# Layer 0's expert products on 64-row TensorE tiles, in two halves around the second scores of a turn

## The chip, the cores and the metric

The kernel runs on one NeuronCore of a Trainium2 chip. The core has TensorE (PE; its weight loads are listed apart as PEld), VectorE (DVE), ScalarE (ACT), GpSimd (POOL) and SyncE (SP, here the issuer of most DMAs). [...] The metric is the device time of one execution in microseconds.

## The reference

Two layers run over x of 16 batches x 512 tokens x 128 channels. In each, the attention part and the feed-forward part read the same normalised x, and their outputs are added to x.

```
xn = layernorm(x)
x  = x + L0_attn(xn) + L0_ffn(xn)      # L0_attn: a memory updated by gradient steps over 8 chunks
xn = layernorm(x)                      # L0_ffn: conv, 16-head attention, norm, 8 dense experts, norm
x  = x + L1_attn(xn) + L1_ffn(xn)      # L1_attn: two causal 16-head attentions with a conv between
                                       # L1_ffn: top 8 of 32 experts, capacity 128
```

The part that the change touches is the dense mixture of layer 0. For each token it is

```
gates = softmax(x1 @ gate_w + gate_b)                       # 8 experts, all are used
y = sum over e of gates[e] * (relu(x1 @ w1[e] + b1[e]) @ w2[e] + b2[e])
```

with w1[e] of 128 x 512 and w2[e] of 512 x 128. Per batch of 512 tokens this is 8 experts, each with two products of 512 x 128 x 512. Everything is fp32.

## The kernel before, in words

**Turns.** The program is written as Python generators ("stages") that a small planner (`Turns.run`, L280) steps once per turn. A stage has a starting turn and a level. In a turn all live stages are stepped in order of level. Level 0 is `tops` with `largest` (L374): the first scores, whose row maxima VectorE takes. Level 1 is `back` with `weighted` (L423): the second scores, their exp on ScalarE, and the products of the exps with the values. Level 2 finishes an attention (`summed`), levels 3 and 4 hold the scan, the projections and norms, and level 6 is `experts0`, the experts of layer 0. TensorE's queue follows this written order (`ORDERED`, L634). The other engines are ordered by the compiler's scheduler, with two written constraints: VectorE's work of level 1 and above stays behind the maxima of the turn (`newest`), and GpSimd's of level 2 and above behind the causal masking (`cleared`).

**Attention.** A head has 8 channels, split into a high and a low part, with the maxima as extra rows. Heads lie in two groups of 64 partitions, so the scores are float32r products on 64-row tiles, one per row group, in pairs (L388 and L465). Layer 0 takes 512 columns a turn. Layer 1 is causal and takes 512, 384, 2 x 256 or 4 x 128 columns, 11 turns for four heads of each row group. The exps are multiplied with the values on 128*32 tiles, four heads beside each other (`values`, L432), several turns later and by four or eight heads at a time (`tail`, L448).

**PSUM.** `pools["ps"]` has eight banks: five slots called `bank`, handed out by `work` (L177), one pair for the second scores (`p2`), one for the value sums (`ctx`). `held` counts the slots kept beyond a turn.

**Experts before.** `ffn(b)` (L530) works on one batch at a time. Its gate is a generator of its own that advances one step per turn. `first(i)` is one 128*128 product of w1 with all 512 tokens (tile phe) and a Relu on ScalarE into hTe. `second(i)` is four 128*128 products of hTe with w2 into pye, which is summed over four units in one bank, multiplied by the gate on ScalarE (L601) and added to `ac` on GpSimd (L602). After the first, units are listed alternately. How many run in a turn is decided by `credit`: each turn adds TURN = 2750 less `load_ns`, an account of the other products of the turn; a unit costs 1000. Units go in pairs, and in turns with value products none go unless more than three are due. They stand last in the turn.

**After the experts.** `middle(b)` waits for the experts of its batch and begins layer 1 for it, one batch per 44 turns. The 32 experts of layer 1 (`moe`) come at the end.

Of the kernel before, what the change touches and what calls it, by code (L numbers as in the profile page):

```python
# [17 lines left out]
P = 128  # L18
# [64 lines left out]
def network(ctx: ExitStack, tc: tile.TileContext, a, out):  # L83
# [39 lines left out]
    gw0 = load(const, "gw0", [P, EXP0])  # L123
# [62 lines left out]
    load_ns, look_ns, array_ns, at_ffn = [0.0], [0.0], [0.0], [-9]  # L186

# [85 lines left out]
    class Turns:  # L273
# [6 lines left out]
        def run(self, until=None):  # L280
            while (self.stages or self.live) and (until is None or not until()):
# [8 lines left out]
                with ExitStack() as behind:  # L290
                    if newest[0] is not None:
                        behind.enter_context(tc.issue_after(newest[0].ins))
                    left += [x for x in self.live if x[0] == 1 and step(x)]
                    if cleared[0] is not None:
                        behind.enter_context(tc.issue_after(cleared[0].ins))
                    left += [x for x in self.live if x[0] > 1 and step(x)]
# [126 lines left out]
    def weighted(slot, vp, c, causal, cn, name):  # L423
# [33 lines left out]
        for i, (kt, n, per, t) in enumerate(widths(causal)):  # L457
# [4 lines left out]
            for u in range(per):  # L462
                for r in range(2):
                    rr = slice(64 * r, 64 * r + 64)
                    mm(sv[:, r, u, :], k[rr, t + u, kt * P : (kt + 1) * P], q[rr, t + u, S - n :])  # L465
            tail(pools["heads"])
# [45 lines left out]
    credit, fetched = [0.0], {}  # L512

    def fetch1(w1, w2, e):
        w1[e] = ff.tile([P, DFF], F32, tag="ew1", bufs=2, name="ew1")
        nc.sync.dma_start(w1[e], a["ew1"][:, e, :])
# [5 lines left out]
    def fetch0(b):  # L522

        x1T = ff.tile([P, S], F32, tag="x1T", bufs=1, name="x1T")
        nc.sync.dma_start(x1T, x1d[1, b])
# [4 lines left out]
    def ffn(b):  # L530
# [12 lines left out]
        def gate():  # L543
            yield from room()
            pgt = hold("pgt")[:, 0 : TB * EXP0].rearrange("p (t e) -> p t e", e=EXP0)
            for t in range(TB):
                mm(pgt[:, t, :], x1T[:, t * P : (t + 1) * P], gw0)
# [22 lines left out]
            y = ff.tile([P, TB, D], F32, tag="y", bufs=2, name="y")  # L570
            nc.scalar.copy(flat(y), pb2)
            nc.gpsimd.tensor_tensor(ac, ac, y, ALU.add)
            yield

        hs, pye, n = {}, [None], 4 * EXP0

        def first(i):
            e, f = divmod(i, 4)
            if e + 1 < EXP0 and f < 2:
                (fetch1, fetch2)[f](w1, w2, e + 1)  # L580
            ph = work("phe")
            mm(ph, w1[e][:, f * P : (f + 1) * P], x1T)
            hs[i] = ff.tile([P, S], F32, tag="hTe", bufs=3, name="hTe")
            nc.scalar.activation(hs[i], ph, AF.Relu, bias=col("fb", i))  # L584
            if i == n - 1 and ("x1", b + 1) in done:
                fetch0(b + 1)

        def second(i):
            e, f = divmod(i, 4)
            h = hs.pop(i)  # L590
            if f == 0:
                pye[0] = toks(hold("pye"))
            for t in range(TB):
                nc.tensor.matmul(  # L594
                    pye[0][:, t, :], lhsT=h[:, t * P : (t + 1) * P], rhs=w2[e][:, f, :],
                    start=(f == 0 and t == 0), stop=(f == 3), skip_group_check=True,
                )
            if f == 3:
                y = ff.tile([P, TB, D], F32, tag="y", bufs=2, name="y")
                for t in range(TB):  # L600
                    nc.scalar.mul(y[:, t, :], pye[0][:, t, :], pr[:, t, e : e + 1])  # L601
                nc.gpsimd.tensor_tensor(ac, ac, y, ALU.add)  # L602
                drop()

        units = [(first, 0)]
        for i in range(1, n):
            units += [(first, i), (second, i - 1)]
        units.append((second, n - 1))
        gating, at = gate(), 0
        while at < len(units):  # L610

            at_ffn[0] = clock[0]
            credit[0] = min(credit[0] + TURN - load_ns[0], 4000)
            more = int(max(credit[0] + 500, 0) // 1000)
            if pools["pairs"]:
                more = more // 2 * 2 if "values" not in locks or more > 3 else 0
            if credit[0] > -2000:

# [984 lines left out]
```

## Time and profile before

| | us |
|---|---|
| runs shown, median (lowest to highest) | 3695.77 (3691.05 to 3702.05) |
| profiled execution, its own time | 3697.03 |
| profiled execution, span of its instructions | 3695.3 |
| TensorE matmuls busy | 3466.2 |
| VectorE busy | 2283.0 |
| ScalarE busy | 2154.0 |
| GpSimd busy | 1571.3 |
| first pye matmul to last | 280.4 to 3104.1 |

Groups of the experts over the whole trace (count, mean of one): phe matmuls of 512 columns, 1024, 612 ns; pye matmuls of 128 columns, 4096, 281 ns; Relu hTe, 512, 690 ns; multiply y, 512, 368 ns; add to ac, 128, 1285 ns. A product in fp32 appears as two passes, each with its own weight load, so 512 phe products make 1024 rows. A float32r product appears as one.

How to read it: a row of the timeline has the start, the length, the engine, the line, the tiles (out<-in), the shape of the TensorE tile as rows*columns, and the count of instructions merged in it. Rows of matmuls overlap, since they include the way through the array. In the groups, the busy time and the mean in ns follow the bar, then the idle time before them and what ended it.

### The profile page before, as it was taken

The page shows a single profiled execution, that of the slowest core. Times are in us where ns is not written, and L with a number is a line of the kernel's source. Part 1 is how long each engine was busy: PE and PEld are TensorE (multiplying, and loading weights), DVE is VectorE, ACT ScalarE, POOL GpSimd, SP SyncE. Part 2 cuts the span into 40 slices and gives each one's busy share as a digit, 9 for nine tenths or more (in the row PEclk, how much of TensorE's full clock was granted, in tenths as well). Part 3 has the DMA queues.
Part 4 walks back from the last instruction along what each step waited for, and adds up shares of the span by engine and source line. Part 5 has one row for each costly group of instructions (what it writes and reads, how often), then busy time and mean ns, then how long its engine had stood idle before and what let it go on. Part 6 is the DMA issues. An engine that isn't in the chain of part 4 may idle for free. (4 is left out here: it accounts for less than half of the span.)

```text
span 3695.3 us, 62879 instructions
## 1 busy us (share of the span) xinstructions
PE 3466.2 (94%) x22209; PEld 1925.9 (52%) x22209; DVE 2283.0 (62%) x5907; ACT 2154.0 (58%) x3703; POOL 1571.3 (43%) x2524
## 2 busy tenths in 40 slices
PE   6999999899999899999999999999999999998877
PEld 3445554454555455455555555555555665443443
DVE  5676656556756565566466666666666666777652
ACT  1556756665656687666566666666666665443433
POOL 5433532442431455432444344434443444443664
PEclk7999999899999999999999999999999999998998
DMA  5222222222223233443434443444344334333343
GB/s 171 68 69 74 80 77 65 68 74 82 65 66 94 85 114 93 122 120 105 135 96 132 121 125 110 120 124 127 101 124 130 114 107 116 96 99 95 84 85 85
DMA packets 290074, 370.83 MB, mean 100 GB/s; under 512 B 46016, under 2 KB 141408, under 8 KB 289376
## 3 DMA queue, kind: packets, MB, share of 16 engines
q1 hardware_dynamic: 282592, 359.99, 34.0%
q0 software_dynamic: 7168, 6.82, 1.1%
q8 instruction: 177, 2.90, 0.3%
q14 instruction: 137, 1.12, 0.1%
HBM read 236.85 MB, written 133.25 MB: 100 GB/s over the span
## 5 line engine op out<-in xcount | busy, mean ns | idle before, releaser
L470 ACT ACTIVATE e<-s 128x1024 f32<-128x1024 f32 (+1 forms) x1216 | 1190.9, 979 | 667.7 <-PE s L196 587.0
L399 DVE TENSOR_REDUCE nm<-s 128x1 f32<-128x512 f32 (+2 forms) x1408 | 906.9, 683 | 527.0 <-PE s L196 525.6
L391 DVE CUSTOM_DVE_ANT_0 s<-s,sb_const 128x512 f32<-128x512 f32 (+1 forms) x1024 | 624.3, 643 | 444.3 <-PE s L196 436.3
L474 POOL TENSOR_SCALAR_AFFINE_SELECT e<-e 128x128 f32<-128x128 f32 (+2 forms) x1408 | 467.0, 367 | 865.9 <-ACT e L470 859.5
L196 PE MATMUL s<-kx,qx 64*128 64x512 f32 (+3 forms) x3072 | 657.3, 430 | 58.8 <-DVE nm L399 14.6
L196 PE MATMUL pc<-e,vp 128*32 128x512 f32 (+3 forms) x6144 | 657.2, 506 | 43.9 <-POOL e L474 41.8
L196 PEld LDWEIGHTS s<-kx,qx 64*128 64x128 f32 x3072 | 293.1, 187 | 627.9 <-issue 251.9
L594 PEld LDWEIGHTS pye<-ew,hTe 128*128 128x128 f32 x4096 | 517.7, 192 | 174.0 <-issue 159.5
L196 PE MATMUL s<-qx,kx 64*128 64x512 f32 (+3 forms) x3072 | 533.2, 360 | 39.4 <-ACT e L470 27.6
L594 PE MATMUL pye<-ew,hTe 128*128 128x128 f32 x4096 | 564.6, 281 | 0.8 <-ACT hTe L584 0.8
L196 PE MATMUL phe<-x1T,ew 128*128 128x512 f32 x1024 | 539.9, 612 | 8.4 <-DVE nm L399 6.4
L584 ACT ACTIVATE hTe<-phe,sb_cols 128x512 f32<-128x512 f32 x512 | 352.8, 690 | 280.5 <-PE phe L196 278.3
L602 POOL TENSOR_TENSOR ac<-ac,y 128x512 f32<-128x512 f32 x128 | 164.5, 1285 | 408.8 <-ACT y L601 380.9
L196 PEld LDWEIGHTS s<-qx,kx 64*128 64x128 f32 x3072 | 294.6, 189 | 82.0 <-ACT e L470 57.0
L398 DVE TENSOR_TENSOR s<-s,sb_const 128x256 f32<-128x256 f32 (+1 forms) x384 | 180.9, 516 | 230.6 <-PE s L196 224.9
L196 PEld LDWEIGHTS pc<-e,vp 128*32 128x32 f32 x6144 | 155.5, 110 | 285.5 <-issue 173.1
L196 PEld LDWEIGHTS phe<-x1T,ew 128*128 128x128 f32 x1024 | 157.7, 192 | 59.8 <-issue 34.2
L601 ACT ACTIVATE y<-pye,pr 128x128 f32<-128x128 f32 x512 | 146.8, 368 | 30.8 <-PE pye L594 25.8
L203 PE MATMUL fill<-sb_pb,sb_const 128*128 128x512 f32 (+2 forms) x324 | 148.4, 547 | 10.9 <-DMA sb_pb<-in_pb 10.3
L391 DVE DVE_READ_ACCUMULATOR2_ANT nm<- 128x1 f32 x1024 | 144.6, 141 | 0.0
L209 POOL TENSOR_SCALAR rs_t<-ss 128x4 f32<-128x4 f32 (+1 forms) x56 | 11.9, 213 | 238.8 <-ACT sq L262 235.1
L209 POOL TENSOR_SCALAR rs_t<-ln_mv 128x4 f32<-128x4 f32 x64 | 12.7, 198 | 178.7 <-DVE ln_mv L219 176.4
(292 smaller groups left out, 3856.0 us busy)
## 6 DMA issues: line engine op xcount, KB each, us to landing
ew<-in_ew SPq DMA_DIRECT2D x256, 256.0 KB
kx<-rk SPq DMA_DIRECT2D x192, 256.0 KB
qx<-rq SPq DMA_DIRECT2D x128, 256.0 KB
rq<-hi SPq DMA_DIRECT2D x64, 256.0 KB
rq<-lo SPq DMA_DIRECT2D x64, 256.0 KB
rk<-hi SPq DMA_DIRECT2D x64, 256.0 KB
rk<-lo SPq DMA_DIRECT2D x64, 256.0 KB
qx<-r SPq DMA_DIRECT2D x64, 256.0 KB
```

Source lines behind the costliest of these rows:

```text
L196: nc.tensor.matmul(o, lhsT=lhsT, rhs=rhs, start=start, stop=stop)
L203: nc.tensor.matmul(o[:, 0:n], lhsT=ident, rhs=cell[0][:, 0:n], start=True, stop=True)
L209: nc.gpsimd.tensor_scalar(t, src, scale, eps, ALU.mult, ALU.add)
L391: newest[0] = nc.vector.tensor_tensor_reduce(out=sv[r][:, 0, :], in0=sv[r][:, 0, :], in1=row["caus"][:, S - n :], scale=1.0, scalar=-BIG, ...
L398: nc.vector.tensor_tensor(dg, dg, bc(row["caus"][:, S - P :], 1, per), ALU.add)
L399: newest[0] = nc.vector.tensor_reduce(nm[:, qt, r, t : t + per], sv[r], AX.X, ALU.max)
L470: nc.scalar.activation(e[:, :, 0 : per * n], s[:, :, 0 : per * n], AF.Exp, scale=SCALE)
L474: cleared[0] = nc.gpsimd.affine_select(out=ev[:, r, :, 0:P], in_=ev[:, r, :, 0:P], pattern=[[0, per], [1, P]], compare_op=ALU.is_ge, fill= ...
L584: nc.scalar.activation(hs[i], ph, AF.Relu, bias=col("fb", i))
L594: nc.tensor.matmul(pye[0][:, t, :], lhsT=h[:, t * P : (t + 1) * P], rhs=w2[e][:, f, :], start=(f == 0 and t == 0), stop=(f == 3), skip_gro ...
L601: nc.scalar.mul(y[:, t, :], pye[0][:, t, :], pr[:, t, e : e + 1])
L602: nc.gpsimd.tensor_tensor(ac, ac, y, ALU.add)
```

## The change

Experts run on 64*128 tiles. For `first`, w1 is laid out so that each group of 64 partitions holds another block of 128 hidden columns, and x1T is loaded twice, once for each row group: the 128 channels are contracted in two steps h = 0, 1. For `second`, each row group contracts its 64 of the 128 hidden rows and sums over the four blocks in a bank of its own. ScalarE multiplies the sum of one bank by the gate, VectorE that of the other, and GpSimd adds both to `ac`. A unit is now (`first` or `second`, expert, half p), 32 per batch instead of 64, and costs 2000 of credit.

A unit is a generator with one yield in its middle. `experts(True)` starts one between levels 0 and 1, if the last turn's credit was over 1000 (`due`), fewer than two slots are held, and, for `second`, the gate has finished (`ready`). `experts()` inside `weighted`, after the second scores and before the value products, runs the rest. At most one unit runs in a turn, in turns with values too. The gate's products use row group 0 alone, in two steps. `y` has half-size tiles, hTe four buffers for three, and some tiles of layer 1 change their pools or tags.

```diff
+    units, running, due, credit = [], [], [False], [0.0]
+    def experts(begin=False):
+        if running:
+            for _ in running.pop():
+                pass
+        elif begin and due[0] and units and held[0] - read[0] < 2:
+            fn, e, p, ready = units[0]
+            if fn.__name__ == "first" or ready:
+                units.pop(0)
+                running.append(fn(e, p))
+                next(running[0])
+                due[0] = False
+                credit[0] -= 2000
...
+                    experts(True)
                     left += [x for x in self.live if x[0] == 1 and step(x)]
+                    experts()
...
                     mm(sv[:, r, u, :], k[rr, t + u, kt * P : (kt + 1) * P], q[rr, t + u, S - n :])
+            experts()
             tail(pools["heads"])
...
-        x1T = ff.tile([P, S], F32, tag="x1T", bufs=1, name="x1T")
-        nc.sync.dma_start(x1T, x1d[1, b])
+        x1T = ff.tile([P, 2, S], F32, tag="x1T", bufs=1, name="x1T")
+        for g in range(2):
+            nc.sync.dma_start(x1T[64 * g : 64 * g + 64], x1d[1, b].rearrange("(h k) s -> k h s", h=2))
...
             for t in range(TB):
-                mm(pgt[:, t, :], x1T[:, t * P : (t + 1) * P], gw0)
+                for h in range(2):
+                    mm(pgt[:, t, :], x1T[0:64, h, t * P : (t + 1) * P], gw0[:, h, :], h == 0, h == 1)
...
-        def first(i):
+        def first(e, p):
+            banks = work("phe"), work("phe")
+            for h in range(2):
+                if p == 0 and e + 1 < EXP0:
+                    (fetch1, fetch2)[h](w1, w2, e + 1)
+                for g in range(2):
+                    rr = slice(64 * g, 64 * g + 64)
+                    nc.tensor.matmul(
+                        banks[g], lhsT=w1[e][rr, h, p, :], rhs=x1T[rr, h, :], start=(h == 0), stop=(h == 1),
+                    )
+                if h == 0:
+                    yield
+            for g in range(2):
+                f = 2 * p + g
+                hs[f] = ff.tile([P, S], F32, tag="hTe", bufs=4, name="hTe")
+                nc.scalar.activation(hs[f], banks[g], AF.Relu, bias=col("fb", 4 * e + f))
...
-        def second(i):
+        def second(e, u):
+            banks = [toks(work("pye")) for _ in range(2)]
+            two = slice(2 * u, 2 * u + 2)
+            for i in range(2):
+                t = 2 * u + i
+                for f in range(4):
+                    for g in range(2):
+                        rr = slice(64 * g, 64 * g + 64)
+                        nc.tensor.matmul(
+                            banks[g][:, i, :], lhsT=hs[f][rr, t * P : (t + 1) * P], rhs=w2[e][rr, f, :],
+                            start=(f == 0), stop=(f == 3),
+                        )
+                if i == 0:
+                    yield
+            y = [ff.tile([P, 2, D], F32, tag="y", bufs=2, name="y") for _ in range(2)]
+            for i in range(2):
+                t = 2 * u + i
+                nc.scalar.mul(y[0][:, i, :], banks[0][:, i, :], pr[:, t, e : e + 1])
+            nc.vector.tensor_tensor(y[1], banks[1][:, 0:2, :], bc(pr[:, two, e], 2, D), ALU.mult)
+            for g in range(2):
+                nc.gpsimd.tensor_tensor(ac[:, two], ac[:, two], y[g], ALU.add)
...
             credit[0] = min(credit[0] + TURN - load_ns[0], 4000)
-            more = int(max(credit[0] + 500, 0) // 1000)
-            if pools["pairs"]:
-                more = more // 2 * 2 if "values" not in locks or more > 3 else 0
...
-            next(gating, None)
+            due[0] = credit[0] > 1000
+            if next(gating, True):
+                ready.append(True)
             yield
```

## The prediction

> **What bounds the kernel now.** I read the page first, then the busy time by stretch, then TensorE's timeline inside one turn, then the waits and the groups by shape. TensorE leads the page:
>
> ```profile
> span 3695.3 us, 62879 instructions
> PE 3466.2 (94%) x22209; PEld 1925.9 (52%) x22209; DVE 2283.0 (62%) x5907; ACT 2154.0 (58%) x3703; POOL 1571.3 (43%) x2524
> ```
>
> By stretch (span cut where layer 0's experts begin, where the scan ends, where the experts end, and where the last `middle` starts):
>
> ```profile
> core 0: us, PE busy (x) PEld busy (x) DVE busy (x) ACT busy (x) POOL busy (x), PEclk, DMA share, GB/s
> 270.00:1530.00 1260.00, 1186.18 (x6856) 648.15 (x6860) 772.19 (x1397) 819.33 (x1600) 509.84 (x496) 0.97 0.28 81
> 1530.00:3110.00 1580.00, 1552.50 (x11052) 918.18 (x11044) 968.64 (x2948) 977.25 (x1563) 653.25 (x1335) 1.00 0.41 118
> 3110.00:3290.00 180.00, 166.89 (x1147) 81.17 (x1147) 134.02 (x414) 87.97 (x110) 74.48 (x188) 0.93 0.40 106
> ```
>
> From 1530 to 3110 us TensorE is busy 98% while VectorE, ScalarE and GpSimd stand at 61, 62 and 41%. So time there is TensorE's time. But its busy rows hide holes. The timeline of two turns, matmuls alone (start, length, ..., count):
>
> ```profile
> 1515.28 0.40 PE L196 MATMUL s<-qx,kx 64*128 64x512 f32 x2
> 1515.60 1.16 PE L594 MATMUL pye<-ew,hTe 128*128 128x128 f32 x8
> 1516.60 1.02 PE L196 MATMUL phe<-x1T,ew 128*128 128x512 f32 x2
> 1517.55 0.51 PE L196 MATMUL s<-kx,qx 64*128 64x512 f32 x2
> 1517.89 0.40 PE L196 MATMUL s<-qx,kx 64*128 64x512 f32 x2
> 1518.21 1.06 PE L196 MATMUL pc<-e,vp 128*32 128x512 f32 x8
> 1519.21 0.50 PE L196 MATMUL s<-kx,qx 64*128 64x512 f32 x2
> ```
>
> Compare ends, since every row carries the same pipeline tail. In unbroken stretches consecutive starts give 0.112 us for a 128-column fp32 pass, 0.43 for a 512-column one (each fp32 matmul is two passes), about 0.23 for a pair of 512-column scores. Scores end at 1515.68 and the eight pye passes at 1516.76: 1.08 for 0.90 of work, so **0.20 us lost** entering 128*128. pye to phe (1517.62) is 0.86 for 0.86: nothing lost. phe to the next scores (1518.06) is 0.44 for 0.23: **0.21 lost** leaving. Scores to scores (1518.29): nothing. Scores to pc: 1519.27, 0.98 for 0.86, 0.12 lost; pc to scores 0.21. So it is the change of tile shape that costs. Measured this way over the whole trace: 64*128 to 128*128 694 times, median 0.200; 128*128 to 64*128 1038 times, median 0.211.
>
> **The change, part by part.**
>
> *Shape switches.* I split TensorE's rows into runs of one shape. 283 runs of 128*128 between scores hold nothing but pye and phe; 39 more follow pc. (150 hold experts and other products, 556 only others; those switches stay.) With the experts on 64*128 the 283 runs vanish, 283 x 0.41 = 116; the 39 lose one switch of two, 39 x 0.20 = 8. **-124 us.** No trace shows fp32 and the scores' float32r alternating in one shape: the price is 0 to 0.20 a switch. I take 0, by pye to phe and pc to pye: same number type with another shape cost 0.20, same shape nothing.
>
> *Array work.* One new unit (a `first` or `second`) replaces one old first plus one old second on average: 512 of them. A `first` is two pairs of products (h = 0, 1; one of each row group), and if the two row groups overlap, 4 pair-passes x 0.43 = 1.72, as two old phe products (4 passes). A `second` is 16 pair-passes x 0.112 = 1.79, as two old pye. Row groups overlap in float32r (the x2 score rows last 0.40, not 0.62, and four-head 128-column score pairs start 0.112 apart, weight loads included); two-pass fp32 overlaps between column tiles (pc, four heads, eight passes: 1.06). The combination is in no row. Here a rule speaks against the change: the Trainium skill, "TensorE: Matmul & The Clock Gate", Part 3, says matmuls start and end in strict order. Then passes a, b of group 0 come before a of group 1: a half of `first` takes three slots, not two, +0.43 x 512 halves = 220, and a half of `second` nine for eight, +0.11 x 512 = 57: +277 us. By that rule pc's eight passes would need five slots, 2.3 us; the row says 1.06. I take the row: 0.
>
> *Banks.* The skill's "TensorEngine Tiling (Array Packing)", Restrictions and Gotchas, Gotcha 1, warns that row tiles write different PSUM banks, so pressure rises. Here: five `bank` slots; the first scores hold two, a unit now two at once (an old one one, and pye one over four turns), so one is spare. By the switches alone the sum below would be -120; with the rule I step one turn. Let t=0 be the end of the second scores in a turn with a `first` and nothing after it. exp starts at 0.20 (its row 1515.71 after scores whose rows end at 1515.68, tail of 0.17 taken off) and the next ScalarE instruction 0.91 later; the second half ends at 0.86; so Relu of group 0 runs 1.11 to 1.80 and its bank is free at about 1.88. TensorE reaches the next unit's first half at 0.86 + 0.23 = 1.09 and lacks one bank: **0.79 late**; with the 384-wide exp (0.81) 0.58. After a `second` (0.37 on ScalarE, 0.42 on VectorE) banks are free at 1.56: 0.47, or 0.26. Mean 0.52. Group 1's matmul blocks all behind it: second scores, values, the next exp. It takes units in consecutive turns, with no values or other product between. Values run in 4 turns of 11 in layer 1 (heads are popped by eights), and credit (+2750 less a turn's loads, -2000 a unit, due over 1000) drops after a unit in a turn with values, so that the next turn stays empty. Stepping it by hand through such cycles gives 3.5 consecutive cases and 2.5 empty turns followed by a unit in 11 turns. 558 turns from 1530 to 3110 make 178 and 127; a quarter of turns have other products, which leaves 134 x 0.52 = **+70**. After an empty turn the bank comes from VectorE's first maximum, 0.20 + 0.69 + 0.14 + 0.08 = 1.11 after the first scores, and TensorE is there after 2 x 0.23: 0.6 late, 95 x 0.6 = **+57**. The kernel before keeps units out of turns with values and has next to no empty turns: its 558 turns (exps counted) hold 466 runs of 128*128 and 91 returns from pc straight to scores. The 134 units before 1530 stand among denser other work: some 28 cases at 0.6, and 10 for ScalarE's longer queue, **+27**. Together 154, 0.30 a unit; the ends are 0 (banks always free) and 0.6 (every unit late).
>
> *Cover.* The first half stands between an exp and the scores waiting for it:
>
> ```profile
> PE s L196 <- ACT e L470: 11.7, 14, 1.2
> ...
> PE s L196 <- ACT e L470: 14.7, 19, 3.7
> ```
>
> (first line 1530 to 3110, second 270 to 1530; total, times, longest.) Of 26 us some go: **-10**, at most -26.
>
> *Gate.* pgt on one row group alone: 16 passes a batch for 8. 128 more x 0.112 = **+14**; nothing hides it.
>
> *Evacuation.* ScalarE keeps 512 Relus and 512 multiplies. VectorE gains 256 multiplies from PSUM at 0.42 = 107 us; GpSimd goes from 128 adds of 1.285 to 512 of half the size, which by the 0.455 of 128x128 and 1.27 of 128x512 I put at 0.72: 369 for 165. Both have the room (61%, 41%), and TensorE hides it; uncovered it would be 310 us. These are the rows by shape:
>
> ```profile
> L398 DVE TENSOR_TENSOR s<-s,sb_const 128x256 f32<-128x256 f32 x256 | 97.9, 427 | 185.0 <-PE s L196 179.5 <-issue 3.8 <-PE fill L203 0.9
> L602 POOL TENSOR_TENSOR ac<-ac,y 128x512 f32<-128x512 f32 x128 | 164.5, 1285 | 408.8 <-ACT y L601 380.9 <-ACT m L415 27.7
> L829 POOL TENSOR_TENSOR eb<-eb,sln 128x128 f32<-128x128 f32 x8 | 3.6, 455 | 0.1
> ```
>
> What is late where it fails: `y` has two buffers and a unit takes both, so a GpSimd queue 2 us behind stops ScalarE's multiply, and with it the exp queued behind: **+5** (0 to 25).
>
> *Pace.* At most one unit a turn, and `second` waits for the gate, some eight turns in which credit stops at 4000: 2.4 turns of credit lost a batch. I expect some 52 turns a batch for 48 now, 12 batches, 48 turns later in all. Now the last batch's experts end 78 turns (exps) before `middle(15)` starts (3110 to 3290), so nothing waits; about 30 units fall where TensorE is busy 93%: **-5**. Beyond 78 turns every turn late would cost 2.3 us.
>
> *DMAs.* SP issues 16 more loads (x1T in two, 512 KB for 256); fetches stay one behind another, now mid-turn, behind the same done matmuls; DMA share is 0.41, and x1T has four turns: 0 (up to 1 us a batch).
>
> **Sum:** -124 + 70 + 57 + 27 - 10 + 14 + 5 - 5 = **+34 us**. The profiled execution took 3697.0 (span 3695.3 and 1.7 around it), 1.2 over the median 3695.8 of the three: 3731 against the first, **3730** against the second. A measurement of this kernel tells about 0.3%, 11 us.
>
> **Rivals.**
> - *Faster* (0.32). One mechanism: units fall mostly where values or other products (60% of turns have some) stand between, and Relu is done in time. Gains 139, less 19 for gate and buffers, leave 120 us: over 512 units **0.23 us each** decides, and I count 0.30. At 0.10 a unit: -69, 3627; at 0.15, 3650; at 0, 3575. For it: the small margin, and waits that hide behind each other. Against it: seven live banks' worth of work on five, in quiet turns.
> - *Bank waits twice over* (0.13). Other work's copies (0.58, as cs or cT) stand ahead of Relu, or VectorE is behind by one multiply (0.42), so 0.45 a unit: +77 more, 3807.
> - *fp32 row tiles do not overlap, or the number types drain* (0.07). +277, or 0.4 on 512 units, +205: 3935 to 4007.
> - *No change* (0.08): waits meet gains, 3685 to 3706.
>
> **How the numbers follow.** The likeliest, 0.40, lies from 3707 to 3775. Slower: 0.40 + 0.13 + 0.07 = 0.60; same 0.08; faster 0.32. The range, 3615 to 3825, takes in the third case and most of the faster one and leaves out about 0.17.
>
> **What would show it.** Right: runs of 128*128 between scores fall by about 300; pye and phe as 64*128 pairs at 0.43 and 0.112; TensorE waits, most of all phe and pye for ACT hTe, ACT y and DVE nm, of 100 to 200 us in sum; turns with values of 3.5 us and more beside empty ones under 1; the last expert some 48 turns later, still before `middle(15)`. Wrong: waits below 0.23 a unit (then faster), pairs at twice these spacings or holes of 0.2 between scores and experts (the fourth case), or `middle` waiting for `ffn`.

## The result, and the profile after

The changed kernel takes 3919.44 us (median of four, 3918.74 to 3921.93). The kernel before, on the same chip, takes 3698.91 (3691.05 to 3703.94). The ratio is **1.0592** [1.058, 1.0605]: 220 us slower. The direction was forecast at 0.60, the size was not: 3730 was forecast, with 3825 as the upper end of the range.

The head of the page after, and the experts' groups (out<-in, count, then busy time and mean, then the idle time before them and its releaser):

```profile
span 3916.9 us, 74084 instructions
...
PE 3593.0 (92%) x27431; PEld 2113.9 (54%) x27431; DVE 2366.7 (60%) x6163; ACT 2121.2 (54%) x3719; POOL 1779.0 (45%) x2924
...
L607 PE MATMUL phe<-x1T,ew 64*128 64x512 f32 x2048 | 689.0, 635 | 44.4 <-DVE h L880 13.3
...
L628 PE MATMUL pye<-ew,hTe 64*128 64x128 f32 x8192 | 636.4, 280 | 48.7 <-ACT y L637 14.4
...
L640 POOL TENSOR_TENSOR ac<-ac,y 128x256 f32<-128x256 f32 x512 | 376.5, 736 | 320.3 <-ACT y L637 256.9
...
L638 DVE TENSOR_TENSOR y<-pye,pr 128x256 f32<-128x256 f32 x256 | 108.1, 422 | 186.8 <-PE pye L628 131.9
```

VectorE's multiply (0.422 us) and GpSimd's add (0.736, estimated at 0.72) cost what was expected of them, and both engines still have room. The busy time by stretch, with the same columns as before:

```profile
core 0: us, PE busy (x) PEld busy (x) DVE busy (x) ACT busy (x) POOL busy (x), PEclk, DMA share, GB/s
270.00:1530.00 1260.00, 1172.79 (x7921) 670.75 (x7922) 766.62 (x1427) 785.09 (x1560) 547.95 (x582) 0.97 0.27 78
1530.00:3110.00 1580.00, 1481.55 (x13198) 939.22 (x13197) 935.75 (x2812) 858.96 (x1412) 720.50 (x1440) 0.97 0.39 109
```

TensorE was busy 1552.50 of the 1580 us from 1530 to 3110 before, and is busy 1481.55 now. It waits more, although the products to be done are the same, and its granted clock there went from 1.00 to 0.97. The loss lies between the starts of the first and the last `middle`, each taken at its first layer norm: that stretch was 1749 us long and is 1939, 190 more. Its row, before and after:

```profile
1549.00:3298.00 1749.00, 1708.38 (x12115) 991.74 (x12112) 1099.28 (x3359) 1058.63 (x1663) 722.92 (x1524) 0.99 0.41 116
1587.00:3526.00 1939.00, 1822.51 (x16126) 1140.14 (x16123) 1175.96 (x3570) 1045.97 (x1688) 880.98 (x1830) 0.97 0.39 108
```

One good and one bad turn in the timeline: TensorE's matmuls, and of VectorE the masks and maxima for which the bad turn waits (start, length, engine, line, tiles, count, and in brackets the idle time and its releaser):

```profile
2506.39 0.51 PE L212 MATMUL s<-kx,qx 64*128 64x256 f32 x4
2506.73 1.02 PE L607 MATMUL phe<-x1T,ew 64*128 64x512 f32 x4
2507.19 0.79 PE L212 MATMUL s<-qx,kx 64*128 64x512 f32 x2
2507.82 1.02 PE L607 MATMUL phe<-x1T,ew 64*128 64x512 f32 x4
2508.77 0.66 PE L264 MATMUL tpc<-sb_const,cs 128*128 128x128 f32 x4
...
2509.36 0.66 PE L212 MATMUL s<-kx,qx 64*128 64x128 f32 x8
...
2509.85 0.45 PE L212 MATMUL s<-qx,kx 64*128 64x512 f32 x2
...
2510.05 1.30 DVE L416 TENSOR_TENSOR s<-s,sb_const 128x512 f32<-128x512 f32 x2 [0.56 <-PE s L212]
...
2510.14 0.62 PE L212 MATMUL s<-kx,qx 64*128 64x512 f32 x2
...
2511.26 1.28 DVE L417 TENSOR_REDUCE nm<-s 128x4 f32<-128x512 f32 x2
...
2512.08 1.26 PE L607 MATMUL phe<-x1T,ew 64*128 64x512 f32 x3 [1.33 <-DVE nm L417]
2512.69 0.66 PE L212 MATMUL s<-qx,kx 64*128 64x384 f32 x1
2513.18 0.59 PE L607 MATMUL phe<-x1T,ew 64*128 64x512 f32 x2
2513.21 0.73 PE L212 MATMUL s<-qx,kx 64*128 64x384 f32 x1
2513.62 1.19 PE L607 MATMUL phe<-x1T,ew 64*128 64x512 f32 x3
2514.73 1.92 PE L212 MATMUL pc<-e,vp 128*32 128x512 f32 x16
```

The first turn is what the change is meant to be. Four phe passes (two steps, two row groups) last 1.02 with the tail, so 0.86 of array time: the row groups overlap. Scores follow them without a hole. In the bad turn, which begins at 2510.14, the unit finds none of the five slots free. Two hold the first scores of this turn, two those of the turn before (2509.36, a turn without a unit), and the fifth holds tpc, which VectorE reads only from 2512.45 on. VectorE adds the masks to both banks of the earlier scores and then takes their maxima one after the other. TensorE is idle for 1.33 us until the first of these banks is read; the second comes one maximum, about 0.6 us, later. So the pair falls apart. The row of three passes is row group 0 with its own two and group 1 with one. The two second scores, which start together in the good turn, start 0.52 apart. From the first phe pass to the next other shape this unit takes 2.65 us, the good one 2.04.

I rebuilt the array's use from the trace (each product's end less the tail of 0.17, its length from its columns, as in the prediction) for the stretch from the first to the last `middle`, 384 units. A hole is time in which no product is on the array. Before, holes make 363 us, of them 256 switches. After, holes make 404: switches are down to 153, and holes directly ahead of an expert product that has no switch went from a few us to 128. And for 236 us, where before there were none, the array works on an expert product of one row group while the other group's half of it stands empty. What one group does alone the other does alone later, so I count half of that, 118 us, as lost. Holes and **stagger** together are 246 us, 0.64 a unit. Of 1,018 halves in the whole trace 628 are more than 0.1 us longer than the 0.86 and 0.89 of an undisturbed one, on average by 0.59.

The waits of that stretch (total, times, longest) say what a unit lacks. First scores (nm), Relus (hTe) and multiplies (y) hold it up in turn:

```profile
PEld phe L607 <- ACT hTe L615: 24.0, 35, 1.3
...
PEld phe L607 <- DVE nm L409: 22.8, 53, 0.9
...
PEld pye L628 <- ACT y L637: 20.3, 38, 0.9
...
PEld phe L607 <- ACT y L637: 16.5, 31, 0.7
...
PEld pye L628 <- DVE nm L409: 13.6, 44, 0.8
...
PE pye L628 <- ACT y L637: 12.9, 36, 0.7
```

### The profile page after: what moved, and what is told of

Its sections match the earlier page's. It is cut to its first block, busy times and chain, and to the rows that moved or that the text cites. A ratio compares the mean times of both kernels' runs of the same rounds, so it can differ in the third digit from the quotient of the medians.

```text
span 3916.9 us, 74084 instructions
## 1 busy us (share of the span) xinstructions
PE 3593.0 (92%) x27431; PEld 2113.9 (54%) x27431; DVE 2366.7 (60%) x6163; ACT 2121.2 (54%) x3719; POOL 1779.0 (45%) x2924
## 5 line engine op out<-in xcount | busy, mean ns | idle before, releaser
L212 PE MATMUL s<-qx,kx 64*128 64x512 f32 (+3 forms) x3072 | 753.2, 434 | 50.6 <-ACT e L489 43.2
L212 PE MATMUL s<-kx,qx 64*128 64x512 f32 (+3 forms) x3072 | 692.3, 431 | 55.8 <-issue 15.7
L607 PE MATMUL phe<-x1T,ew 64*128 64x512 f32 x2048 | 689.0, 635 | 44.4 <-DVE h L880 13.3
L628 PE MATMUL pye<-ew,hTe 64*128 64x128 f32 x8192 | 636.4, 280 | 48.7 <-ACT y L637 14.4
L628 PEld LDWEIGHTS pye<-ew,hTe 64*128 64x128 f32 x8192 | 584.6, 191 | 102.1 <-ACT y L637 23.2
L640 POOL TENSOR_TENSOR ac<-ac,y 128x256 f32<-128x256 f32 x512 | 376.5, 736 | 320.3 <-ACT y L637 256.9
L212 PEld LDWEIGHTS s<-qx,kx 64*128 64x128 f32 x3072 | 355.7, 192 | 139.6 <-ACT e L489 88.9
L607 PEld LDWEIGHTS phe<-x1T,ew 64*128 64x128 f32 x2048 | 289.3, 195 | 186.2 <-issue 47.8
L615 ACT ACTIVATE hTe<-phe,sb_cols 128x512 f32<-128x512 f32 x512 | 324.0, 685 | 18.8 <-PE phe L607 17.3
L638 DVE TENSOR_TENSOR y<-pye,pr 128x256 f32<-128x256 f32 x256 | 108.1, 422 | 186.8 <-PE pye L628 131.9
```

The source lines that it names most:

```text
L212: nc.tensor.matmul(o, lhsT=lhsT, rhs=rhs, start=start, stop=stop)
L607: nc.tensor.matmul(banks[g], lhsT=w1[e][rr, h, p, :], rhs=x1T[rr, h, :], start=(h == 0), stop=(h == 1),)
L615: nc.scalar.activation(hs[f], banks[g], AF.Relu, bias=col("fb", 4 * e + f))
L628: nc.tensor.matmul(banks[g][:, i, :], lhsT=hs[f][rr, t * P : (t + 1) * P], rhs=w2[e][rr, f, :], start=(f == 0), stop=(f == 3),)
L640: nc.gpsimd.tensor_tensor(ac[:, two], ac[:, two], y[g], ALU.add)
```

## The experiments

Two theories stood against each other at the start. **A:** a unit asks for two of five `bank` slots at once while the first scores hold two more, so it waits for a bank, and the row groups fall out of step. **B:** the new place in the turn and the new planner are at fault: units go into turns with values, quiet turns go empty and wait for exp. **C**, the chain of y buffers and GpSimd, was kept as a third.

**First scores in one bank.** In both kernels the first scores, maxima and masks of row group 1 are left out; VectorE takes both maxima from one bank.

```diff
-            sv = [work("s1")[:, 0 : per * n].rearrange("p (i n) -> p i n", i=per) for r in range(2)]
+            sv = [work("s1")[:, 0 : per * n].rearrange("p (i n) -> p i n", i=per)] * 2
...
-                for r in range(2):
-                    rr = slice(64 * r, 64 * r + 64)
-                    mm(sv[r][:, u, :], q[rr, t + u, qt * P : (qt + 1) * P], k[rr, t + u, :n])
+                mm(sv[0][:, u, :], q[0:64, t + u, qt * P : (qt + 1) * P], k[0:64, t + u, :n])
+                load_ns[0] += 0.5 * (0.45 * n + 105)
...
```

> The changed kernel, but the first scores are computed for row group 0 alone, into one bank; VectorE takes both row groups' maxima from it. Left out: row group 1's first scores and, for its maxima, the causal mask, so the maxima of half of the heads are another head's. TensorE's time for the first scores stays, since the two row groups run beside each other; VectorE's work falls by some 0.1 to 0.2 us a turn. Theory A (five bank slots: a unit's two and the first scores' two leave one spare, so units wait for each other's evacuation, about 0.7 us a unit): a slot more is free and the waits of phe and pye mostly go: 3600 to 3720 us. Theory B (placement: units in turns with values leave quiet turns empty, and these wait for exp and maxima): the loss stays, 3850 to 3920. Theory C (the two y buffers and GpSimd's adds hold ScalarE): stays, 3870 to 3920.

> Control: the same edit in the kernel before (first scores of row group 0 alone, one bank, both maxima from it; left out as in the other). Its experts hold one bank for phe and one for pye, so there is no shortage to relieve: A, B and C all expect 3670 to 3705 us. Were it to fall by over 60, the edit itself (less VectorE work) would be the gain, and the other run could not speak for A.

The changed kernel fell by 201 to 3717.93 (ratio to before 1.006 [1.0037, 1.0082]), the control by 35 to 3663.25 (0.9899 [0.9877, 0.992]; a little below what was expected, since VectorE masks less). About 165 us hang on the bank. The two are still 55 apart.

**Both halves after the second scores.**

```diff
+                    left += [x for x in self.live if x[0] == 1 and step(x)]
                     experts(True)
-                    left += [x for x in self.live if x[0] == 1 and step(x)]
...
+            experts(True)
             experts()
```

> The changed kernel with both halves of a unit after the second scores, ahead of the values; same tiles, same planner. The unit's banks are taken 0.86 + 0.23 = 1.1 us later and released about 0.8 later, and exp is ready before the Relus. A: waits shrink by 0.2 to 0.3 us a unit, 3790 to 3860. If the split around the second scores covers a wait for exp that matters, it is slower than 3919. B and C: 3900 to 3935.

3882.84 (1.0509 [1.0488, 1.0529]), between A's range and the others. The row groups keep step better (an expert product alone for 134 us, not 236), but the scores now wait for exp in turns that a unit's first half had covered. In its waits from its first to its last `middle`:

```profile
PEld s L212 <- ACT e L490: 127.1, 136, 1.4
PE s L212 <- ACT e L490: 78.6, 111, 1.1
```

These were 28.6 and 10.6 in the changed kernel. Under the new planner the first half is worth more as cover than the 10 us that the prediction gave it.

**Tiles alone.** 64-row tiles and new layouts, but whole units at the end of a turn by the old credit rules.

```diff
-                    experts(True)
                     left += [x for x in self.live if x[0] == 1 and step(x)]
-                    experts()
...
-            experts()
...
-            due[0] = credit[0] > 1000
+            more = int(max(credit[0] + 500, 0) // 1000)
+            if pools["pairs"]:
+                more = more // 2 * 2 if "values" not in locks or more > 3 else 0
+            if credit[0] > -2000:
+                more = max(more, int((look_ns[0] - load_ns[0] - 400) / 1000 + 0.7))
+            for _ in range(more // 2):
+                due[0] = True
+                experts(True)
+                experts()
```

> The 64-row tiles alone: a unit runs whole, at the end of a turn, under the rules of the kernel before (credit rounded to pairs, none in turns with values unless more than three are due, the look at VectorE's time). The switches saved stay saved (about -124). A: units then follow each other in quiet turns with 0.46 us of scores between, and the next needs a bank freed 0.97 after the last: 0.5 on some 280 units, +140: 3690 to 3780. B: the loss came with the placement, so it goes: 3570 to 3640.

3790.6 (1.0251 [1.0223, 1.0278]), just above A's range and far from B's: the tiles alone make the kernel slower by 93 us, though they save 135 us of switches.

**The emission alone.** The new order and planner with the old 128-row products: a first unit takes its two banks one by one, a second unit needs one bank.

```diff
-            banks = work("phe"), work("phe")
-            for h in range(2):
+            banks = []
+            for g in range(2):
...
+                banks.append(work("phe"))
+                nc.tensor.matmul(banks[g], lhsT=w1[e][:, f * P : (f + 1) * P], rhs=x1T, start=True, stop=True)
...
-            banks = [toks(work("pye")) for _ in range(2)]
+            bank = toks(work("pye"))
```

> The new order of emission alone: a unit in the middle of the turn, half before and half after the second scores, at most one a turn, by the new planner rule; but with the old products on all 128 rows and the old layouts, so that a unit of the first kind asks for its two banks one after the other (one in each half) and a unit of the second kind needs one bank and one y. Every half is now a 128*128 run of its own between 64-row scores: some 1,000 such runs where the kernel before has 283, at the 0.41 us in and out read from the trace of before, so switches cost about 300 us more than before and 440 more than in the changed kernel. Theory A (two banks a unit are what hurts): waits for banks fall to 0.2 to 0.4 us a unit, 150 to 250 us less, so 4100 to 4210 us. Theory B or C (the place in the turn, or the chain behind the units): the waits stay, 4300 to 4400.

3921.13 (1.0604 [1.0586, 1.0622]): as slow as the changed kernel, for another reason, and faster than either theory said. Its switches came near what was expected, 745 us from 270 us to the last `middle` against 355 in the changed kernel and 492 before. So all else is 390 us cheaper than in the changed kernel, 0.76 a unit where I had expected 0.3 to 0.5. Against the kernel before, switches cost 253 more and the time is 223 to 226 more: **but for its switches, the new place in the turn costs nothing when a unit takes one bank at a time**. Theory B in its plain form falls with this run.

**Units kept out of turns with values.** Placement alone, in the changed kernel:

```diff
-        elif begin and due[0] and units and held[0] - read[0] < 2:
+        elif begin and due[0] and not (clock[0] in coming and credit[0] < 3500) and units and held[0] - read[0] < 2:
...
-            yield
+            if len(old) >= pools["heads"]:
+                coming.add(clock[0] + 1)
+            yield
+        coming.add(clock[0] + 1)
```

> The changed kernel (3919 us), but the planner keeps a unit out of a turn that carries value products unless 3,500 ns of room are saved up, where the changed kernel lets any turn take one. Everything else as changed. Theory A (a unit lacks free banks wherever it stands, because both its banks are asked for while the first scores hold two): little or nothing, 3890 to 3980. Theory B (the changed planner puts the units in the wrong turns, so quiet turns go empty and wait for exp): 3750 to 3850.

3823.22 (1.0332 [1.0309, 1.0355]): 96 us gained, as B had said and A, as I had put it, had not. By the rebuilt array most of it is A's waits: holes ahead of the experts fall from 128 to 84 us and stagger from 118 to 95, together 67 of the 70 us by which the stretch between the first and last `middle` got shorter. Placement decides how many units find no bank; I had taken that number for fixed.

**Tiles alone, first scores in one bank** (both edits above; same part left out).

> 64-row tiles with whole units at the end of a turn under the old planner (3791 us in its own run), and the first scores from row group 0 alone in one bank, as in s1_one_bank (row group 1's first scores, their maxima and masks are left out; the control, the kernel before with the same part left out, took 3663). Theory A: with a bank free the tiles show their gain, 124 to 136 us of switches, less the waits that remain: 3560 to 3660, that is at or below its control. If the tiles' price is not in the banks (exp covered less, the row groups' own work): 3680 to 3760.

3685.71 (0.9973 [0.9951, 0.9995]), 22 above its control in medians. Near the lower end of the second case: a free bank takes most of the 93 us away, but the gain of the switches still doesn't appear.

**Emptying a first unit earlier.** Two ways. By token halves, so that Relu can begin in the middle of the unit:

```diff
+            for x in range(2):
+                xs = slice(256 * x, 256 * x + 256)
...
+                        nc.tensor.matmul(
+                            banks[g][:, xs], lhsT=w1[e][rr, h, p, :], rhs=x1T[rr, h, xs], start=(h == 0), stop=(h == 1),
+                        )
...
+                    nc.scalar.activation(hs[f][:, xs], banks[g][:, xs], AF.Relu, bias=col("fb", 4 * e + f))
```

> The changed kernel, but a unit of the first kind does both row passes of tokens 0 to 255 before the second scores and of tokens 256 to 511 after them (the same columns in all), and each half's Relu is issued on ScalarE with it, so that ScalarE's part of the emptying starts a half earlier, in two instructions of 256 columns a bank (an estimate: 0.43 us each by half of the 685 ns row plus about 0.1, so about +0.18 a bank, +90 us of ScalarE work in all). Theory A: banks come free 0.4 to 0.7 us earlier behind half the units: 3830 to 3880. Theory B or C: no change or the dearer Relu, 3910 to 3960.

4057.77 (1.0975 [1.0957, 1.0993]), a miss in the other direction. The second half writes other columns of the banks that Relu is reading, and the program's dependencies make it wait for that Relu. Its waits from the first to the last `middle`:

```profile
PEld phe L611 <- ACT hTe L616: 87.7, 174, 1.8
...
PE phe L611 <- ACT hTe L616: 26.0, 72, 1.4
```

24.0 and 4.9 in the changed kernel. Nine in ten of the weight loads' waits for Relu stand ahead of a second half. In this program a bank is one thing to wait for, whatever columns are used. The other way is to let VectorE do the Relu of row group 1, in three of the kernels:

```diff
-                nc.scalar.activation(hs[f], banks[g], AF.Relu, bias=col("fb", 4 * e + f))
+                if g == 0:
+                    nc.scalar.activation(hs[f], banks[g], AF.Relu, bias=col("fb", 4 * e + f))
+                else:
+                    nc.vector.tensor_scalar(hs[f], banks[g], col("fb", 4 * e + f), 0.0, ALU.add, ALU.max)
```

> The changed kernel, but the Relu of row group 1's bank is done by VectorE (add the bias, maximum with 0) instead of ScalarE, so that it doesn't stand behind exp and the other Relu: its bank comes free up to 0.7 us earlier behind a unit of the first kind, of which there are 256, while VectorE, which also empties the first scores, gets 256 instructions of about 0.69 us. Theory A, with ScalarE's queue as what holds the bank: 3850 to 3890. If VectorE's maxima are held up as much as ScalarE gains: 3905 to 3935.

> Units kept out of turns with value products unless 3,500 ns are saved up (3823 us in its own run), and row group 1's Relu on VectorE. Theory A: each unit now follows a unit or values, so ScalarE's queue is the last holder of a bank more often than the maxima: 3750 to 3790. Otherwise 3810 to 3840.

> 64-row tiles with whole units at the end of a turn under the old planner (3791 us), and row group 1's Relu on VectorE. Theory A: 3735 to 3770, still above the kernel before, since units of the second kind and the waits for exp are as they were. Otherwise 3780 to 3810.

3914.55 (1.0594 [1.0561, 1.0628]), 3833.77 (1.0361 [1.0329, 1.0394]) and 3771.7 (1.02 [1.0169, 1.023]), against ratios of 1.0592, 1.0332 and 1.0251 without the edit: nothing, no change clear of the noise, and a gain of about 19 us, just above A's range. In the first of them the waits of phe for Relu are nearly as they were:

```profile
PEld phe L607 <- DVE nm L409: 23.3, 54, 0.9
...
PEld phe L607 <- ACT hTe L616: 21.9, 25, 1.3
```

The bank whose Relu ScalarE does is needed too, and for that one nothing has changed. In the changed kernel a faster reader for one of two banks doesn't help a unit that needs both.

**Row group 0 alone in the units.** Row group 1's products are left out, and both readers take row group 0's bank, so all other work stays.

```diff
-            banks = work("phe"), work("phe")
+            banks = [work("phe")] * 2
...
-                for g in range(2):
+                for g in range(1):
...
```

> The changed kernel (3919 us), with row group 1's products of both kinds left out: a unit writes one bank. The second Relu and VectorE's multiply read row group 0's bank instead, so ScalarE's, VectorE's and GpSimd's work, the planner, the place in the turn and the y buffers stay as they are; and since the two row groups overlap, the array's time of an undisturbed half stays too (0.86 and 0.89 us). Theory A (the second bank, with the stagger of the row groups that it brings): the waits fall from 0.67 to 0.70 us a unit to the 0.1 to 0.2 that one-bank units show, 512 x 0.5 = 250 us, and the time to 3640 to 3720. If it is the place in the turn, the planner or the chain of y buffers and GpSimd: 3850 to 3920.

3831.61 (3815.3 to 3848.91; ratio 1.0369 [1.0318, 1.0421]): neither. The row of the stretch says why it can't decide:

```profile
1530.00:3110.00 1580.00, 1499.82 (x10376) 923.03 (x10374) 981.83 (x2939) 905.38 (x1473) 754.88 (x1516) 0.93 0.39 114
```

With half of the array empty in the experts the granted clock is 0.93 there instead of 0.97, and over the whole run 0.926 instead of 0.957. An estimate: 3824.64 x 0.926 / 0.957, as if all of the profiled execution's time went with the clock, is 3701. This probe takes work off the array and with it changes the clock, so what it shows is not the bank's price.

**Five slots against six.** The probe that settles more: in all of these the second scores of row group 1 are left out, and exp reads row group 0's bank twice. That sets one bank free. It stays unused in the five-slot runs, and is given to the shared slots in the six-slot runs. The work is then the same within a pair, and the clock nearly so.

```diff
-            s = pools["ps"].tile([P, 2, 512], F32, tag="p2", bufs=pools["p2"], name="s2")
+            s = pools["ps"].tile([P, 1, 512], F32, tag="p2", bufs=pools["p2"], name="s2")
...
-            nc.scalar.activation(e[:, :, 0 : per * n], s[:, :, 0 : per * n], AF.Exp, scale=SCALE)
+            nc.scalar.activation(e[:, :, 0 : per * n], bc(s[:, 0, 0 : per * n], 1, 2), AF.Exp, scale=SCALE)
```

and, in the six-slot runs alone:

```diff
-        return pools["ps"].tile([P, 512], F32, tag="bank", bufs=5, name=name)
+        return pools["ps"].tile([P, 512], F32, tag="bank", bufs=6, name=name)
```

> Control for the next run. The changed kernel with the second scores of row group 1 left out: exp reads row group 0's bank twice, so its work stays, and the time the planner counts for the turn stays. The second scores then need one bank instead of two; here the bank set free stays unused, and the five slots that first scores and units share stay five. The array's time in row group 0 stays, and less of the array is busy, which lowered the granted clock from 0.957 to 0.947 to 0.951 with halved first scores: 3880 to 3960.

> As the control before it, with the bank set free given to the shared slots: six instead of five, nothing else. First scores and two units in a row then have a bank each. Theory A (the wait for a bank, with the stagger of the row groups that it brings, is what the change costs): most of the 0.67 to 0.70 us a unit goes, 200 to 300 us below the control, 3620 to 3720. If the cost is the place in the turn, the planner, ScalarE's queue as such or the chain of y buffers and GpSimd: within 60 us of the control.

> The kernel before with the same part left out (second scores of row group 1, exp reads one bank twice) and five slots: what leaving it out does by itself. Array time of row group 0 as it was, clock a little lower: 3690 to 3760.

> The kernel before, same part left out, with six slots: what a sixth bank is worth to one-bank units. Its trace of before shows next to no waits of TensorE for banks, so 0 to 20 us below its five-slot control. Theory A: the sixth bank is worth ten times as much to the changed kernel.

The changed kernel: 3861.05 with five slots (ratio to before 1.0456 [1.0434, 1.0478]), **3716.07** with six (1.0063 [1.0046, 1.008]), at clocks of 0.952 and 0.951. The kernel before: 3681.69 (0.9972 [0.9952, 0.9991]) and 3660.94 (0.9914 [0.9893, 0.9936]), at 0.966 and 0.960. One bank more is worth 145 us to the changed kernel and 21 to the one before. That is somewhat under the 200 to 300 expected, and well outside the 60 that the other theories allowed. The waits of the experts with five slots, and with six, each from the first to the last `middle`:

```profile
PEld phe L608 <- DVE nm L409: 22.8, 53, 0.9
PEld phe L608 <- ACT hTe L616: 21.7, 30, 1.3
PEld pye L629 <- ACT y L638: 20.0, 38, 0.8
...
PEld phe L608 <- ACT y L638: 16.2, 32, 0.6
...
PE pye L629 <- ACT y L638: 12.4, 35, 0.6
```

```profile
PEld phe L608 <- DVE nm L409: 8.5, 23, 0.5
...
PEld pye L629 <- ACT y L638: 1.2, 3, 0.6
...
PEld phe L608 <- ACT hTe L616: 1.0, 4, 0.6
...
PE pye L629 <- ACT y L638: 0.4, 1, 0.4
...
PEld phe L608 <- ACT y L638: 0.2, 1, 0.2
```

The waits of phe for Relu and multiply and of pye for multiply are all but gone, so these were waits for the bank and not for ScalarE's data. Two runs more with six slots ask what is left:

> 64-row tiles with whole units at the end of a turn under the old planner (3791 us with all the work and five slots), with row group 1's second scores left out and six slots, as in the pair before. Its controls are the kernel before with the same part left out: 3682 with five slots, 3661 with six. If the bank is all that stands between the tiles and their gain of 124 us less 14 for the gate: 3560 to 3640. If other terms eat the gain (row groups out of step, waits for exp in the turns without a unit): 3650 to 3720.

> Units in the middle of the turn but kept out of turns with value products unless 3,500 ns are saved up (3823 us with all the work and five slots; 96 below the changed kernel), with row group 1's second scores left out and six slots; the changed kernel with that took 3716. If the placement had won its 96 us by making fewer units wait for a bank, a sixth bank leaves little of it: 3690 to 3730. If placement and banks are separate costs, both gains add: 3610 to 3650.

3686.66 (0.9945 [0.9927, 0.9964]) and 3664.57 (0.9902 [0.9884, 0.992]). Placement wins 52 us in medians with a sixth bank, 96 without: between the two expectations, so part of its gain was the banks and part is its own. Against the kernel before with six slots (0.9914) both are level within the intervals. Even with a spare bank the tiles gain nothing.

**The runs on one scale.** Time over the kernel before (or over the control with the same part left out), as difference of the ratios times 3699 us; switches measured in both traces from 270 us to the last `middle`; the rest over 512 units:

| | time | switches | rest | rest per unit |
|---|---|---|---|---|
| changed kernel | +219 | -137 | 356 | 0.70 |
| five slots, second scores halved | +179 | -136 | 315 | 0.62 |
| both halves after the second scores | +188 | -145 | 333 | 0.65 |
| out of value turns | +123 | -158 | 281 | 0.55 |
| tiles alone, old planner | +93 | -135 | 228 | 0.45 |
| first scores in one bank | +60 | -130 | 190 | 0.37 |
| six slots | +55 | -138 | 193 | 0.38 |
| tiles alone, first scores in one bank | +27 | -142 | 169 | 0.33 |
| tiles alone, six slots | +12 | -145 | 157 | 0.31 |
| out of value turns, six slots | -4 | -151 | 147 | 0.29 |
| emission alone, 128 rows | +223 | +253 | -30 | -0.06 |

The last two columns hold everything that is not a switch: waits, stagger, clock, cover and the gate. In this table the versions on 64-row tiles with five slots and all of the work pay 0.45 to 0.70 a unit; with a bank to spare it is 0.29 to 0.38, wherever in the turn the units stand; on 128 rows nothing is left. Two runs that are not in it lie outside these bounds (estimates, with the switches of the version that each was made from): tiles alone with VectorE's Relu at 0.41, and token halves, with their waits for Relu, at 0.97.

## Why the prediction was wrong in size

**Switches: right.** Forecast -124; the trace shows 492 us of them before and 355 after, -137. Alternating number types in one tile shape leave no hole, as was assumed. (The first hole read in the prediction is 1.08 less 0.90, 0.18 and not 0.20; its sum rests on the medians, and stays.)

**Array work: right in an undisturbed half, incomplete elsewhere.** Row groups overlap in fp32 (four phe passes in 0.86 us, a quarter of all phe halves at that length): group 1's first pass starts together with group 0's first and 0.43 us ahead of group 0's second, though group 0's product is written first. So the strict order of starts that the Trainium skill states ("TensorE: Matmul & The Clock Gate", Part 3) is not what this trace shows. The third rival falls by its own marks, though its 3935 lies near the measured time. But "0" holds only when both groups have their banks.

**Banks: this is the step that failed, by its size.** It put 154 us, 0.30 a unit, with 0.6 as the upper end; what stands in its place is 0.64 a unit in the rebuilt trace, and 0.70 with all that is no switch. The mechanism was the right one: the break-even of 0.23 was passed, and the sixth slot took 145 us away. What the step left out:
- It ended with the arrival of the late bank. In the trace the groups stay apart afterwards, through the second scores and the second half. The holes alone are 128 us over 384 units, 0.33, close to the 0.30; the stagger adds as much again, 118 us, 0.31.
- It counted one late event in about half of the units, and the holes bear that out: some 220 of about 0.5 us stand in or ahead of first halves of the 384 units. But a unit that starts out of step stays so: 62% of the halves are long, second halves (316) as often as first ones (312).
- It took 1.11 us for the first bank to come back from VectorE, from a fused mask and maximum. In the turns with 256 or 128 columns mask and maximum are separate, and in the turn shown the masks of two banks (1.30 us) stood before two maxima (1.28), and tpc held the fifth bank: the wait was 1.33, not 0.6. That is one turn, not the mean.

The second rival (0.45 a unit, 3807) had the right sign of the error and still fell short.

**Cover: within its bound against the kernel before, too small under the new planner.** The prediction read the matmuls' waits for exp alone; the weight loads' stand beside them (50.3 us between the first and the last `middle`). In the two rows, which can count one wait twice, the scores' waits for exp went from 62 to 39 us. But taking the first half away from its place raised them to 206, and still that version was faster by 37.

**Evacuation and y buffers: right for the changed kernel.** From the first to the last `middle` ScalarE's multiply waited 3.5 us for GpSimd's add and VectorE's 20.6, and the sixth slot, which leaves this chain as it was, took most of the loss away. In some probes the chain does hold ScalarE (below). **Pace: right.** The last batch's experts are stored at 3388, and the first layer norm of its `middle` starts at 3526, so nothing waited there. **Gate and DMAs** were not tried separately.

**Clock: not in the sum.** It was 0.99 between the first and the last `middle` before and is 0.97 now: 0.02 x 1939 gives at most some 40 us, an estimate, and contained in the holes and lengths above. No run isolates it.

**What stays open.** With a spare bank 0.29 to 0.38 us a unit remain and eat the gain. In these probes one row group does fewer scores than the other, which itself sets the groups apart by the 0.23 us of a pair in every turn, so they can't show how far a kernel with all its scores and enough banks would come. Halves are still long in them, so stagger has its part, but no run separates it from the clock, from waits for exp and from GpSimd. With tiles alone and six slots the scores wait for exp more than in the kernel before (50.3 and 11.7 there):

```profile
PEld s L212 <- ACT e L487: 88.8, 124, 11.1
...
DVE y L636 <- POOL ac L638: 56.2, 30, 13.1
...
PE s L212 <- ACT e L487: 51.9, 80, 10.9
...
ACT y L635 <- POOL ac L638: 17.3, 3, 12.6
```

The longest of these waits is the chain that the prediction named under evacuation: while GpSimd worked on layer norms from 1611 us on, ScalarE's multiply waited 12.6 us for its add, and the second scores waited 11.1 us for the exp behind that multiply.

No version with all of the work beat the kernel before; the nearest is tiles alone with VectorE's Relu, 3771.7.

## What to carry to other kernels

When a product is split over two row groups, count the banks it needs at the same moment as well as the array time it saves: a unit that needs two of them starts with the first and is done with the last, and between the two half of the array stands idle. To price a buffer, give the same program one more of it and compare with the same pair of the kernel before; taking work out to free a buffer moves other things (here the granted clock, from 0.957 to 0.926). A planner's placement and the number of buffers are one question, since placement decides who finds a buffer free.

## What the runs showed of the hardware

The granted clock was lower where less of the array was used, though TensorE was busy no less: with one row group left out of the experts it was 0.93 from 1530 to 3110 us (busy 1499.82), with both 0.97 (busy 1481.55). In the kernel before it was 1.00, with 1552.50 us busy. Row groups of TensorE run apart when one of them waits: a float32r score of one group and fp32 expert passes of the other are on the array at the same time, and a pair of scores that normally starts together started 0.52 us apart.
